# Transposes of the last keys and queries on the way back from DRAM, and first loads behind weight loads

## The chip, the core and the metric

The kernel runs on one core of a Trainium2 chip. The core has five engines with a queue of instructions each: TensorE (PE, with its weight loads PEld), VectorE (DVE), ScalarE (ACT), GpSimd (POOL) and SyncE (SP). Each works through its own queue in order, and they wait for each other by semaphores. The metric is the device time of one execution in microseconds (us).

## The reference, cut to what matters

```
xn = layernorm(x)                                  # x: 1024 x 512
q, k, v = xn @ Wq.T, xn @ Wk.T, xn @ Wv.T          # 32 heads of queries, 8 of keys and values, 128 wide
q, k = rmsnorm(q, q_norm_w), rmsnorm(k, k_norm_w)  # per head
scores = q @ k.T / sqrt(128)                       # 4 heads of queries share one head of keys
attn = softmax(scores + slope[head] * (key - query), causal)
s = (attn @ v) @ Wo.T
gate, up, down = dequantized 4-bit weights         # 512 x 1792, 512 x 1792, 1792 x 512
g = silu((silu(xn @ gate) * (xn @ up)) @ down)
out = x + s * g
```

All of it is computed near float32 accuracy. Where TensorE multiplies in 16 bits, both factors are split into a high and a low part, and three matmuls (high-high, high-low, low-high) are summed (`mm3`, lines 112 to 116). Keys, queries, values and probabilities therefore come as pairs of 16-bit tiles.

## The kernel before, in words

The order of the instructions on every engine is written out by hand: each queue holds what the program issues, in that order. There are four stages: the layer norm and the gated network (to about 207 us), the projections (from 211 us), a stretch in which the last two projections and the first scores of attention take turns (from about 429 us), and attention alone (from about 480 us).

*Projections.* There are twelve, numbered k = 0 to 11: four rounds of one for keys and values of two groups ("kv", lines 695 to 698) and two for queries of one group each ("q"). A group is one head of keys with its four heads of queries. Number 9 is the last for keys and values (groups 6 and 7), number 10 the queries of group 6, number 11 those of group 7. Each goes through 8 tiles of 128 rows: TensorE makes a tile of 128x512, ACT copies it out and sums squares, POOL multiplies by the inverse norm, and DVE splits it into a high and a low half in one 16-bit tile `a16` (`halves`, lines 667 to 682), which has five buffers. A step later SP issues a DMA that transposes this tile from SBUF to SBUF (`transposed`, L686), and two steps after that a plain DMA that stores the transposed tile in DRAM (`store`, L691 for queries into `qd`, L693 for keys into `kd`). Projection 11 differs: its pairs stay in SBUF (`last_pairs`) and are transposed into place when they are needed (`last_queries`, L855).

The weights of projection k + 2 are loaded during projection k, a quarter with each of the tiles 0 to 3 (L509), and ACT takes their squares from tile 5 on (L517). Squares, copies and the weights' own split into high and low (L578 on ACT, L580 on DVE) stand in ACT's one queue in the order of the tiles. Before the first tile of projection 9 the program loads the keys, the values and the first block of queries of group 0 (lines 1140 to 1144).

*Attention.* Per group it goes through blocks of 256 queries, in an order such as 2, 3, 0, 1 (group 0: 3, 2, 1, 0), four heads each, two tiles of 128 queries per head: 256 steps. In a step TensorE makes the scores of one tile (`s<-kT,qT`), and products of probabilities and values (`av<-pT,vT`) and of the output projection (`op`) of earlier steps. DVE adds the bias and finds the minimum (L916), ACT takes exponentials (L922) and the high half (L941), DVE the low half (L950), and SP issues a DMA that transposes the pair from SBUF to SBUF (`split_lo`, L958; L953 for block 0). The values' products come 9 steps after the scores and need the transposed probabilities `pT`. Steps in block 3 transpose 14 and 16 blocks of 128x128, in block 2 10 and 12, in blocks 1 and 0 at most 8.

Keys of the next group are loaded at the fifth step of a group (`load_keys`, L837, 512 KB), values later (`load_values`, L841, 512 KB), and queries block by block ahead of their use (`load_queries`, L845, 512 KB). Weights of the output projection come in quarters (`wor`, L872, 256 KB), are scaled by POOL (L875) and split by ACT (L881) and POOL (L882).

SP issues every DMA of the kernel, loads, stores and transposes. A transpose is issued only when its source is ready, and what stands behind it in SP's queue waits with it. `defer(n, f)` puts an instruction n steps later in this order.

Of the kernel before, what the change touches and what calls it, by code (L numbers as in the profile page):

```python
# [12 lines left out]
F16 = mybir.dt.float16  # L13
# [8 lines left out]
P = 128  # L22
# [3 lines left out]
HKV = 8  # L26
NH = 4
HD = 128
FF = 1792
NI = FF // P  # L30
NT = S // P
# [4 lines left out]
NQT = QB // P  # L36
# [40 lines left out]
def attention_gated_by_ffn_kernel(ctx, tc, x, gu_w, gu_z, gu_s, dn_w, dn_z, dn_s, wq, wkv, wo, qnw, knw, out):  # L77
    nc = tc.nc
    ve, se, ge, te, sp = nc.vector, nc.scalar, nc.gpsimd, nc.tensor, nc.sync

    const = ctx.enter_context(tc.tile_pool(name="const", bufs=1))
    dram = ctx.enter_context(tc.tile_pool(name="scratch", bufs=1, space=DRAM))
# [54 lines left out]
    gsT = const.tile([P, NI, 2, KT], F32, name="gsT")  # L137

    kd = [dram.tile([P, 2, NT, 2 * HD], F16, name=f"kd{i}") for i in range(HKV // 2)]
    vd = [dram.tile([P, NT, 2 * HD], F16, name=f"vd{g}") for g in range(HKV)]  # L140
    qd = [dram.tile([NT, P, 2 * NH * HD], F16, name=f"qd{g}") for g in range(HKV)]
    ald = [dram.tile([1, 2 * HD], F32, name=f"ald{i}") for i in range(HKV // 2)]
# [343 lines left out]
    def finish_step():  # L486

        for f in finishing.pop(clock[0], ()):
            f()
        clock[0] += 1  # L490

    def defer(steps, f):
        finishing.setdefault(clock[0] + steps, []).append(f)
# [4 lines left out]
    class Projection:  # L498
# [168 lines left out]
        def halves(self, t):  # L667
            f = self.f[t // HT][:, t % HT]
            n = self.n
            if self.kind == "q":  # L670
                a16 = fq.tile([P, 2, n, HD], F16, tag="a16", name=f"q16_{self.i}_{t}", bufs=5)
                hi, lo = a16[:, 0], a16[:, 1]
            else:
                a16 = fq.tile([P, 2, 2, HD], F16, tag="a16", name=f"k16_{self.i}_{t}", bufs=5)
                hi, lo = a16[:, :, 0, :], a16[:, :, 1, :]
                ve.tensor_tensor(f, f, wn.unsqueeze(1).to_broadcast([P, 2, HD]), ALU.mult)
            ve.tensor_copy(hi, f)
            ve.tensor_tensor(lo, f, hi, ALU.subtract)
            if self.k == len(projections) - 1:
                last_pairs[t] = a16  # L680
            else:
                defer(1, lambda: self.transposed(t, a16))

# [11 lines left out]
    projections = []  # L695
# [4 lines left out]
    def prepare(k, t):  # L700

        if k < len(projections):
            p = projections[k]
            if t == -1:
                for i in range(p.n + 1):
                    p.squares(i)
            elif t == 1:
                p.norms()
            elif t == 2:
                p.scale()  # L710
            elif t == 6:
                p.factors()
            if 2 <= t < 2 + p.n:
                p.split_head(t - 2)
            elif p.kind == "kv" and 4 <= t < 6:
                p.split_values(t - 4)
# [86 lines left out]
    def queue_half(p, half):  # L803

        last = p is projections[-1]

        def due(steps, i, f):
            if last and i is None:
                c = TILES + LAST_ROOTS[half]
            elif last:  # L810
                c = TILES + LAST_PAIRS[half * HT + i] - 4
            else:
                c = clock[0] + (i or 0)
            finishing.setdefault(c + steps, []).append(f)

        due(0, None, lambda: p.inverse(half))
        if p.by_root:
            due(1, None, lambda: p.root(half))
            due(2, None, lambda: p.newton(half, True))
        else:  # L820
            for i in range(3):
                due((i + 1) // 2, None, lambda i=i: p.newton(half, i == 0))
        later = int(p.by_root)
        for i in range(HT):
            t = half * HT + i
            due(4 + later, i, lambda t=t: p.halves(t))
            due(2 + later, i, lambda t=t: p.normalize(t))

    NB = S // QB
    blocks = [(g, qbs) for g in range(HKV) for qbs in (FIRST_ORDER if g == 0 else ORDER if g < HKV - 1 else LAST_ORDER)]  # L830
    units = [(g, qb, hh) for g, qbs in blocks for hh in range(NH) for qb in qbs]
    kT, vT, qT, woh, wol = {}, {}, {}, {}, {}
    trel, pT, oT, wor = {}, {}, {}, {}

    def load_keys(g):
        kT[g] = ap1.tile([P, NT, 2, P], F16, tag="kT", name=f"kT{g}")
        sp.dma_start(kT[g].rearrange("p t a k -> p t (a k)"), kd[g // 2][:, g % 2])  # L837

    def load_values(g):
        vT[g] = ap1.tile([P, NT, 2, HD], F16, tag="vT", name=f"vT{g}")  # L840
        sp.dma_start(vT[g].rearrange("p t a d -> p t (a d)"), vd[g])  # L841

    def load_queries(g, qb):
        qT[g, qb] = ap1.tile([P, NQT, 2, NH, P], F16, tag="qT", name=f"qT{g}_{qb}", bufs=2)
        sp.dma_start(  # L845
            qT[g, qb].rearrange("p t a g q -> p t (a g q)"), qd[g][qb * NQT : (qb + 1) * NQT].rearrange("t p c -> p t c")
        )
# [11 lines left out]
    def wo_squares_sums():  # L859
        ve.tensor_tensor(rvs, rv, rv, ALU.mult)  # L860
        ve.tensor_tensor(swo16, rvs, swo, ALU.mult)
# [22 lines left out]
    def relative(g):  # L884

        rel = trel[g] = ap1.tile([P, S], F32, tag="trel", name=f"trel{g}")
        if g == 0:
            ge.iota(rel, pattern=[[-1, S]], base=S - P, channel_multiplier=1, allow_small_or_imprecise_dtypes=True)
            ge.affine_select(rel, rel, pattern=[[-1, S]], compare_op=ALU.is_ge, fill=1e20, base=S - P, channel_multiplier=1)
            ge.tensor_scalar(rel, rel, rc, float(SLOPES[NH - 1]), ALU.mult, ALU.mult)  # L890
        else:
            ge.tensor_scalar(rel, trel[g - 1], float(SLOPES[g * NH + NH - 1] / SLOPES[g * NH - 1]), None, ALU.mult)
# [176 lines left out]
    def early_tile(c):  # L1069

        if c % 2 == 0:
            scores(*at(c // 2))
        for stage, lag in ((biased, 1), (exponentials, 2), (split_hi, 5), (split_lo, 6)):
            if (c - lag) >= 0 and (c - lag) % 2 == 0:
                advance(stage, (c - lag) // 2)

    def step(n):
        nonlocal last_ps
        if n < nn:
            u, qt = order[n]  # L1080
            g, qb, hh = units[u]
            for due in q_at.get(n, ()):
                if due[0] < HKV - 1:
                    load_queries(*due)
            for t, due in LAST_QUERIES.items():
                if due == n:
                    last_queries(t)
            if g + 1 < HKV:
                if n % (NB * BS) == KEYS_STEP:
                    relative(g + 1)  # L1090
                    load_keys(g + 1)
                elif n % (NB * BS) == VALUES_STEP:
                    load_values(g + 1)
            scores(u, qt)
# [42 lines left out]
    last_ps = None  # L1137
    relative(0)
    for k, p in enumerate(projections):
        if k == len(projections) - 3:  # L1140
            load_keys(0)
            load_values(0)
            for qb in blocks[0][1]:
                load_queries(0, qb)
        for t in range(NT):
            prepare(k + 1, t)
            if k + 2 < len(projections):
                if t < KT:
                    projections[k + 2].load(t)
                n = projections[k + 2].n  # L1150
                for i in (range(n + 1)[: n // 2], range(n + 1)[n // 2 : n - n // 4], range(n + 1)[n - n // 4 :])[t - 5] if t >= 5 else ():
                    projections[k + 2].squares(i)
            if t == HT:
                p.undo()
            if (k, t) == (len(projections) - 3, HT + 1):
                wo_squares_sums()

            row = t if k < len(projections) - 1 else (t + HT) % NT
            p.tile(row)
            finish_step()  # L1160
            if t % HT == HT - 1:
                queue_half(p, row // HT)
            c = (k - len(projections) + 2) * NT + t
            if c >= 0:
                for due in q_at.get(c // 2, ()) if c % 2 == 0 else ():
                    load_queries(*due)
                if c == 2 * KEYS_STEP:
                    relative(1)
                    load_keys(1)
                early_tile(c)  # L1170
# [46 lines left out]
```

## Time and profile before

| | |
|---|---|
| median of 3 runs | 1058.47 us (1057.25 to 1058.75) |
| the profiled execution | 1057.9 us |
| its span, first to last instruction | 1056.1 us |
| mean granted TensorE clock | 0.989 |
| busy share PE, DVE, ACT, POOL | 95%, 83%, 76%, 40% |
| mean traffic of the DMAs | 195 GB/s, 205.43 MB |
| packets under 512 bytes | 401538 of 456095 |

The profile is of one execution. Times within it count from its first instruction. "Busy" is the time in which an engine works on an instruction, waits not included; for SP the rows are the issues of DMAs ("SPq"), and their duration is the time that the issue took, not the transfer. A line number such as L958 is the line of the kernel; a name such as pT<-p is the tile written and the tile read, and stands for all buffers of that name. The share of the DMAs is the mean busy time of 16 DMA engines; it can be above 1 where packets overlap. The chain of waits follows the work that ended last back from the end, at each step to what released it.

### The profile page before, as it was taken

The numbers are of one execution on the slowest core, as the hardware profiler recorded it, in microseconds if no ns is written. First come the engines' busy times: TensorE is split into PE (matmuls) and PEld (weight loads), VectorE is DVE, ScalarE is ACT, GpSimd is POOL, SyncE is SP. The second block draws the span as 40 slices with busy tenths as digits, with TensorE's granted clock in tenths as the row PEclk, the third lists the DMA queues.
The fourth block names the chain that finished last, engine by engine and source line by source line (L and its number), as shares of the span: only waits on it lengthen the run. The fifth ranks groups of instructions, "written<-read, shape, count | busy, mean of one in ns | idle before, by whom it ended". The sixth has DMA issues, their size and how long they took to land.

```text
span 1056.1 us, 18372 instructions
## 1 busy us (share of the span) xinstructions
PE 1001.2 (95%) x5909; PEld 585.6 (55%) x5909; DVE 878.1 (83%) x1744; ACT 800.9 (76%) x2160; POOL 423.7 (40%) x408
## 2 busy tenths in 40 slices
PE   7899999999999999997899999999999999998996
PEld 4344487744444444444556566567666665665563
DVE  7988997537878886786789898798998989978985
ACT  5777745868887786877779788787987979967772
POOL 2587762125655644461225215113151141340632
PEclk9999999999999999899999999999999999999998
DMA  7123269446999989989999899899999998999995
GB/s 244 60 90 124 75 200 327 148 149 138 243 234 215 258 195 259 225 172 237 200 191 217 187 222 198 165 223 209 187 222 180 227 210 172 232 226 168 236 187 130
DMA packets 456095, 205.43 MB, mean 195 GB/s; under 512 B 401538, under 2 KB 412094, under 8 KB 455998
## 3 DMA queue, kind: packets, MB, share of 16 engines
q1 hardware_dynamic: 455998, 204.26, 87.1%
q8 instruction: 46, 0.75, 0.3%
q14 instruction: 51, 0.42, 0.1%
HBM read 78.37 MB, written 27.27 MB: 100 GB/s over the span
## 4 chain that ended last, share of the span: by engine, by line
PE 63%; DVE 11%; DMA 9%; ACT 9%; issue 6%; POOL 1%; SPq 0%; DVEq 0%; POOLq 0%; ACTq 0%
DMA pT<-p 6%; PE gu_ps L273 5%; PE s L114 4%; PE s L116 4%; PE s L115 4%; PE ps_q L115 4%; PE av L114 4%; PE ps_q L116 4%; PE ps_q L114 4%; PE av L116 4%; PE av L115 4%; PE op L116 4%; PE op L114 4%; PE op L115 4%; PE ps_kv L114 2%
## 5 line engine op out<-in xcount | busy, mean ns | idle before, releaser
L950 DVE SCALAR_TENSOR_TENSOR p<-pf,row,p 128x1024 f16<-128x1024 f32 (+7 forms) x256 | 223.4, 873 | 24.5 <-ACT p L941 21.5
L922 ACT ACTIVATE pf<-pf,row 128x1024 f32<-128x1024 f32 (+7 forms) x256 | 197.4, 771 | 41.1 <-DVE row L916 36.7
L916 DVE CUSTOM_DVE_ANT_0 pf<-s,trel,cs 128x1024 f32<-128x1024 f32 (+7 forms) x256 | 207.0, 809 | 21.3 <-PE s L116 20.7
L941 ACT ACTIVATE p<-pf,row 128x1024 f16<-128x1024 f32 (+7 forms) x256 | 196.6, 768 | 9.5 <-DMA pT<-p 4.6
L114 PE MATMUL av<-pT,vT 128*128 128x256 f16 (+1 forms) x640 | 168.8, 264 | 23.8 <-DMA pT<-p 23.8
L115 PE MATMUL av<-pT,vT 128*128 128x256 f16 (+1 forms) x640 | 168.8, 264 | 0.0
L116 PE MATMUL av<-pT,vT 128*128 128x256 f16 (+1 forms) x640 | 168.6, 264 | 0.0
L114 PE MATMUL s<-kT,qT 128*128 128x512 f16 (+3 forms) x384 | 126.2, 329 | 5.7 <-DVE row L916 5.7
L115 PE MATMUL s<-kT,qT 128*128 128x512 f16 (+3 forms) x384 | 126.0, 328 | 0.0
L116 PE MATMUL s<-kT,qT 128*128 128x512 f16 (+3 forms) x384 | 124.4, 328 | 0.0
L875 POOL TENSOR_SCALAR wor<-wor,rvs 128x512 f32<-128x512 f32 x32 | 51.8, 1618 | 173.2 <-DMA wor<-in_wo 152.6
L115 PE MATMUL ps_q<-wl_q,xth 128*128 128x512 f16 x256 | 98.0, 383 | 3.8 <-DVE wl_q L580 3.8
L114 PEld LDWEIGHTS <-vT 128*128 128x128 f16 x640 | 62.9, 98 | 64.3 <-DMA pT<-p 16.8
L116 PE MATMUL ps_q<-wh_q,xtl 128*128 128x512 f16 x256 | 98.0, 383 | 0.0
L114 PE MATMUL ps_q<-wh_q,xth 128*128 128x512 f16 x256 | 97.8, 382 | 0.0
L114 PE MATMUL op<-woh,oh 128*128 128x512 f16 x248 | 94.8, 382 | 0.0
L116 PE MATMUL op<-woh,ol 128*128 128x512 f16 x248 | 94.7, 382 | 0.0
L115 PE MATMUL op<-wol,oh 128*128 128x512 f16 x248 | 94.6, 382 | 0.0
L984 ACT ACTIVATE oh<-av 128x256 f16<-128x256 f32 x128 | 47.8, 374 | 57.8 <-PE av L116 57.1
L115 PEld LDWEIGHTS <-vT 128*128 128x128 f16 x640 | 63.0, 98 | 42.4 <-issue 4.4
L665 POOL TENSOR_TENSOR f_q<-f_q,inv_q 128x512 f32<-128x512 f32 x64 | 80.1, 1276 | 1.1
L882 POOL TENSOR_TENSOR wol<-wor,woh 128x512 f16<-128x512 f32 x32 | 50.3, 1572 | 62.2 <-ACT woh L881 60.4
(195 smaller groups left out, 2259.6 us busy)
## 6 DMA issues: line engine op xcount, KB each, us to landing
qd<-tr_q SPq DMA_DIRECT2D x56, 256.0 KB, 3.1
qT<-qd SPq DMA_DIRECT2D x28, 512.0 KB, 4.4
wq<-in_wq SPq DMA_DIRECT2D x32, 256.0 KB, 4.1
wo_sq<-in_wo SPq DMA_DIRECT2D x8, 1024.0 KB, 8.4
wor<-in_wo SPq DMA_DIRECT2D x32, 256.0 KB, 3.6
gui<-in_gu_w SPq DMA_DIRECT2D x13, 512.0 KB, 3.5
wkv<-in_wkv SPq DMA_DIRECT2D x16, 256.0 KB, 3.8
vd<-v SPq DMA_DIRECT2D x8, 512.0 KB, 4.7
```

The costliest lines, as they stand in the source:

```text
L114: te.matmul(ps, lhsT=lh, rhs=rh, start=first, stop=False)
L115: te.matmul(ps, lhsT=lh, rhs=rl, start=False, stop=False)
L116: te.matmul(ps, lhsT=ll, rhs=rh, start=False, stop=last)
L273: te.matmul(banks[j][:, k, :], lhsT=w[:, j, ws], rhs=x[:, j, k * 512 : k * 512 + 512], start=x is xth, stop=x is xtl)
L665: ge.tensor_tensor(f, f, ib, ALU.mult)
L875: ge.tensor_scalar(wor[g, i], wor[g, i], rvs[:, g : g + 1], None, ALU.mult)
L882: ge.tensor_tensor(wol[g, i], raw, woh[g, i], ALU.subtract)
L916: ve.tensor_tensor_reduce(p, ps, trel[g][:, S - w :], cs[:, hh : hh + 1], 3e38, ALU.add, ALU.min, least[:, c])
L922: se.activation(p, p, AF.Exp, bias=least[:, c], scale=-1.0, accum_out=total[:, c])
L941: se.activation(p16[u, qt][:, :, 0, :], pf[u, qt], AF.Copy, scale=scale[:, qt : qt + 1])
L950: ve.scalar_tensor_tensor(lo, p, scale, hi, ALU.mult, ALU.subtract)
L984: se.activation(oh, av_ps[u], AF.Copy, scale=1.0 / P_SCALE)
```

## The change

Three places are edited.

1. In `halves`, the pairs of projections 9 and 10 are no longer transposed from SBUF to SBUF. The tile `a16` is stored as it is: that of projection 9 into a new DRAM tensor `kn`, that of projection 10 into `qd[6]`.
2. `load_keys` for groups 6 and 7 issues eight DMAs that transpose out of `kn`, one in each of eight steps, each for 128 keys of one group (2 blocks of 128x128), instead of one plain load. `load_queries` for group 6 issues two transposes of 8 blocks out of `qd[6]` for each block of 256 queries, instead of one plain load.
3. The loads of group 0's keys and of its first queries move from before the first tile of projection 9 to its fifth tile, behind the four weight loads of projection 11. The load of group 0's values moves to the fifth tile of projection 10.

```diff
     kd = [dram.tile([P, 2, NT, 2 * HD], F16, name=f"kd{i}") for i in range(HKV // 2)]
+    kn = dram.tile([NT, P, 2 * 2 * HD], F16, name="kn")
...
             if self.k == len(projections) - 1:
                 last_pairs[t] = a16
+            elif self.k >= len(projections) - 3:
+
+                dst = qd[self.i][t] if self.kind == "q" else kn[t]
+                defer(1, lambda: sp.dma_start(dst, a16.rearrange("p a g d -> p (a g d)")))
             else:
                 defer(1, lambda: self.transposed(t, a16))
...
     def load_keys(g):
         kT[g] = ap1.tile([P, NT, 2, P], F16, tag="kT", name=f"kT{g}")
+        if g // 2 == HKV // 2 - 1:
+            for t in range(NT):
+                defer(t, lambda t=t: sp.dma_start_transpose(kT[g][:, t], kn[t][:, g % 2 * 2 * HD : (g % 2 + 1) * 2 * HD]))
+            return
         sp.dma_start(kT[g].rearrange("p t a k -> p t (a k)"), kd[g // 2][:, g % 2])
...
         qT[g, qb] = ap1.tile([P, NQT, 2, NH, P], F16, tag="qT", name=f"qT{g}_{qb}", bufs=2)
+        if g == HKV - 2:
+            for i in range(NQT):
+                sp.dma_start_transpose(qT[g, qb][:, i].rearrange("p a g q -> p (a g) q"), qd[g][qb * NQT + i])
+            return
...
     for k, p in enumerate(projections):
-        if k == len(projections) - 3:
-            load_keys(0)
-            load_values(0)
-            for qb in blocks[0][1]:
-                load_queries(0, qb)
         for t in range(NT):
...
             if t == HT:
                 p.undo()
+                if k == len(projections) - 3:
+                    load_keys(0)
+                    for qb in blocks[0][1]:
+                        load_queries(0, qb)
+                elif k == len(projections) - 2:
+                    load_values(0)
```

## The prediction

> **What bounds the kernel now.** I read the page's engine line, then the stretches with their granted clock, then TensorE's timeline for its idle times, then the chain of waits around the first of them, and last the timeline of the SP queue, which issues every DMA.
>
> ```profile
> PE 1001.2 (95%) x5909; PEld 585.6 (55%) x5909; DVE 878.1 (83%) x1744; ACT 800.9 (76%) x2160; POOL 423.7 (40%) x408
> ```
>
> TensorE is the bound: 95% busy, so time can come only from its idle times and from stretches at a low clock. The timeline of TensorE has these beside the lines of this change (the bracket is the idle time before the row and what ended it):
>
> ```profile
> 423.94 0.58 PE L115 MATMUL ps_q<-wl_q,xth 128*128 128x512 f16 x1 [3.83 <-DVE wl_q L580]
> 493.33 0.27 PE L114 MATMUL av<-pT,vT 128*128 128x256 f16 x1 [3.25 <-DMA pT<-p]
> 502.17 0.28 PE L114 MATMUL av<-pT,vT 128*128 128x256 f16 x1 [2.75 <-DMA pT<-p]
> 508.74 0.28 PE L114 MATMUL av<-pT,vT 128*128 128x256 f16 x1 [2.80 <-DMA pT<-p]
> 532.35 0.27 PE L114 MATMUL av<-pT,vT 128*128 128x256 f16 x1 [1.22 <-DMA pT<-p]
> 867.01 0.28 PE L114 MATMUL av<-pT,vT 128*128 128x256 f16 x1 [0.81 <-DMA pT<-p]
> 936.41 0.27 PE L114 MATMUL av<-pT,vT 128*128 128x256 f16 x1 [1.47 <-DMA pT<-p]
> ```
>
> The stretches (length, busy time of PE, PEld, DVE, ACT, POOL, then clock, DMA share, GB/s) add a second cost of a stall: the clock after it.
>
> ```profile
> 490.00:500.00 10.00, 6.17 (x37) 3.92 (x35) 5.24 (x12) 5.27 (x10) 2.84 (x3) 0.83 1.06 270
> 500.00:510.00 10.00, 5.03 (x41) 3.82 (x42) 4.45 (x9) 5.29 (x12) 4.95 (x4) 1.00 1.18 173
> ```
>
> The chain of waits (start, duration) shows what is behind the first stall, and the SP queue's timeline why that DMA was late:
>
> ```profile
> 416.15 4.23 DMA wq<-in_wq
> 420.40 0.73 ACT sq_q L517 x2
> 423.19 0.71 DVE wl_q L580
> ```
>
> ```profile
> 402.67 1.08 SPq L837 DMA_DIRECT2D kT<-kd  x1
> 403.80 0.42 SPq L841 DMA_DIRECT2D vT<-vd  x1
> 404.27 0.43 SPq L845 DMA_DIRECT2D qT<-qd  x1
> 404.81 0.40 SPq L509 DMA_DIRECT2D wq<-in_wq  x1
> 405.96 2.96 SPq L686 DMA_TRANSPOSE tr_q<-q  x1
> ...
> 416.15 0.70 SPq L509 DMA_DIRECT2D wq<-in_wq  x1
> ...
> 493.05 2.99 SPq L958 DMA_TRANSPOSE pT<-p  x1
> ...
> 497.19 4.60 SPq L958 DMA_TRANSPOSE pT<-p  x2
> ```
>
> Three loads of 512 KB stand ahead of the four weight loads of the last projection; the transposes behind them take 2.96 us to issue instead of 1.32, the fourth weight load goes out at 416.15, and ScalarE, which reached its squares at 413.95, waits until 420.40. From 450 to 533 the SP queue has hardly a gap, and the transposes of probabilities in it are late: those that DVE finished at 487.6 and 491.8 go out at 497.19 and 502.62, 9.6 and 10.8 us later. TensorE's four stalls from 493 to 513 wait for exactly these.
>
> **What the change does to the queues.** The order on PE, DVE, ACT and POOL is the same in both kernels. On SP, 16 transposes go between 434 and 488 (8 tr_kv, 8 tr_q) while the 16 stores stay, from another tile; three first loads move behind the weight loads (values a projection later); six plain loads (two kT, four qT, 820 to 935) become 16 transposes of 2 blocks (128x128) and 8 of 8 blocks, out of DRAM. They wait for stores that landed over 300 us earlier and for buffers freed as before, so no wait is added but for SP's own time; POOL issues no DMA. The price of an issue is in the rows by line (ns minimum/median/maximum):
>
> ```profile
> L686 SPq DMA_TRANSPOSE tr_q<-q x56: 1246/1324/2962, 259.1 to 486.7; - x56
> L686 SPq DMA_TRANSPOSE tr_kv<-k x32: 1188/1247/2435, 236.7 to 462.6; - x32
> L837 SPq DMA_DIRECT2D kT<-kd x8: 570/574/1079, 402.7 to 890.3; - x8
> ```
>
> **Part 1, weights ahead of first keys: -5.9.** From 402.67, three rounds of weight load, store and transpose (0.57 + 0.52 + 1.37 with gaps) put the fourth weight load at 410.1; landing 4.23 later it is there at 414.3. ScalarE's wait of 6.45 us shrinks to 0.4. TensorE's 3.83 goes, and so does the slow clock behind it: 12 matmuls from 423.94 at 0.43 us apart instead of 0.215, 2.5 us. 6.3 less the 0.4. Keys and queries go out at 412.6 and 413.2, with the 7.5 us that qT took in the old burst they land at 420.7; the first scores are due at 419.74 + 2.6 = 422.3. Cover 1.6 us; if it is gone, the first scores wait by the difference. Values land near 445, wanted at 480: nothing.
>
> **Part 2, 16 transposes out of the SP queue: -10.1.** Behind the SP gap that ends at 450.14 stand 3 tr_kv and 8 tr_q: 3 x 1.30 + 8 x 1.37 = 14.9 us with gaps, more than the 10.8 us of lateness, so the pT transposes go out when DVE is done. Stalls 3.25 + 2.75 + 2.80 + 0.34 (512.84) + 1.22 go, and the clock of 0.83 over 10 us, 1.7: 12.1. ScalarE's three waits of 2.51, 2.51 and 2.64 for POOL's scaled wor in the same place go too, since the wor loads stand in the same queue. Late next is the chain of ACT and DVE: in 480 to 540 they are busy 42.8 and 42.0 us, in 48 us that would be 89% on average, but 510 to 520 has ACT at 9.37 of 10 already, and three small stalls for DVE row L916 stand between 479 and 489 (0.74, 0.68, 0.28). I give back a little more than these 1.7: 2.0.
>
> The Trainium skill's page "TensorE: Matmul & The Clock Gate" (Why this matters for your kernels) allows idle gaps up to about 3 us without a loss of clock. By that rule the stall of 2.56 us at 660.21 would have kept the full clock, and it did not: 660 to 680 was granted 0.91; the gaps of 2.75 and 2.80 kept it. The row decides: a gap near 2.5 us may cost 1.7 us or nothing.
>
> **Part 3, what comes later: +5.0, the unknown.** The SP queue around the loads of keys:
>
> ```profile
> 850.55 8.31 SPq L958 DMA_TRANSPOSE pT<-p  x3
> 858.95 0.54 SPq L845 DMA_DIRECT2D qT<-qd  x1
> 859.58 6.07 SPq L958 DMA_TRANSPOSE pT<-p  x2
> ...
> 926.24 0.80 SPq L845 DMA_DIRECT2D qT<-qd  x1
> 927.15 7.03 SPq L958 DMA_TRANSPOSE pT<-p  x2
> ```
>
> From 841 to 865 and from 912 to 940 SP issues without a break, so lateness carried into these stretches is not worked off, and the stalls at 867.01 and 936.41 wait for their last transposes: their slack is zero. All depends on x, the issue time of a transpose out of DRAM, which no row shows. In group 5 the keys' eight fall between 822.3 and 841.3, 19 us: eight pT at 1.40 are 11.2, two wor and a qT 2.4, free 5.4; needed 8(x + 0.05). In group 6, 891 to 910: 11.2 and 1.5 taken, free 6.3; needed 10(x + 0.05), two of them queries; and right ahead of 927.15 the load of 0.80 becomes two transposes. With x at the plain load's 0.574 the sums are 5.0, 6.2 and +0.4: 0.4 us late. With x at the transposes' 1.25 and 1.32: 5.0 late in group 5, 6.8 + 1.9 = 8.7 in group 6, with clock (1.7 and 2.5, as above) 17.9. The instruction is nearest to the second row, the source and the 2 blocks to the first; 4 and 8 blocks cost nearly alike (1.25, 1.32), so what is paid is the kind of access. I lean to the first and take 0.7: 0.6 + 1.2 + 0.7 = 2.5 us late, plus one clock dip, 1.7. DMA time: the stretch 440 to 450 ran at 0.51 share and 132 GB/s, 2.0 us for 512 KB, six of them 12.1; 96 blocks at 0.15 (14 and 16 blocks go out in 4.5 us back to back) are 14.4. +2.3 over 110 us whose DMA share is already above 1; a third of it, 0.8, on the path. Together 5.0. No gain is likely here; at best the missing 512 KB bursts (pT took 1.96 and 2.58 behind one) make it 0.
>
> The skill's page "DMA: Bandwidth & Descriptors" (Why small descriptors are slow) speaks against this part: SBUF to SBUF escapes, but 256-byte pieces against HBM pay 11 cycles for 8. No row here has a transpose out of DRAM; by it, as an estimate, the 14.4 would be 19.8, and the forecast 1049.3 at the same third.
>
> **Sum.** -5.9 - 10.1 + 5.0 = -11.0 against the profiled execution's 1057.9 (span 1056.1 and 1.8 around it): 1046.9. That execution lies 0.6 under the median of the runs, so 1047.5.
>
> **Rivals.** (1) Slower: a transpose out of DRAM holds SP as long as one in SBUF or longer. For: the kind of instruction, and 32 rows that never fall below 1.19. Against: those 32 have both ends in SBUF. At 1.25 the 17.9 eats the 16.0: 1060.4. It decides from x of about 1.2; at 1.6 it would be 1067. (2) The stalls at 493 to 513 turn into waits for ACT and DVE: the small stalls for DVE row L916 stand just ahead of them. Against: ACT's own waits there come from the SP queue. Then half of part 2: 1052.5. (3) Part 1 does not do what it says: keys or queries of the first block miss 422.3, as SP is 5 to 10 us behind at 402 to 420. Then a wait of some 3 us there: 1050.5.
>
> **How the numbers follow.** Chances: forecast 0.50 (1040 to 1052), rival 1 0.32, rival 2 0.12, rival 3 0.06. Range: low, all of 6.3 and 12.1 with nothing given back, 1040, less 1 for the unknown; high, rival 1's own value, 1061. Left out is mostly x above 1.25 or slow packets, 0.15. Forecast, 2 and 3 are faster by over 0.2% (2.1 us, about what a measurement can tell): 0.68. Rival 1 lies around no change: 0.07 same, 0.25 slower. The likeliest one's own range is 1040 to 1052.
>
> **What would show it.** Right: no idle time of TensorE before the ps_q that stood at 423.94, ScalarE's wait for wq under 1 us; no pT stalls over 1 us between the first av and the second group's; pT issued within 2 us of DVE's end there; rows kT<-kn and qT<-qd as transposes under 0.8 us. Wrong: those rows at 1.2 us or more and stalls of 4 us and more where 867.01 and 936.41 stood, with a clock under 0.95 there; or landings of those transposes far over 4 us.

## The result

The changed kernel takes 1067.05 us (median of 4 runs, 1064.66 to 1070.91), the kernel before beside it 1057.86 us. The ratio is 1.0081 with a 95% interval of 1.0054 to 1.0107: it is 0.8% slower. A second set of runs (run 5 below) gave 1.0071 (1.0043 to 1.0098). The prediction was 1047.5 us with a range of 1039 to 1061: a gain was forecast and a loss came, above the range. The profiled execution took 1064.66 us, the least of the four; its span is 1062.9 us.

The first half of the prediction can be read off the timeline of TensorE after the change. These are its idle times for `pT` (the bracket: us, what ended it), first in the stretch that held the stalls of 2.75 to 3.25 us, then in groups 5 and 6:

```profile
488.03 0.28 PE L114 MATMUL av<-pT,vT 128*128 128x256 f16 x1 [0.36 <-DMA pT<-p]
494.32 0.28 PE L114 MATMUL av<-pT,vT 128*128 128x256 f16 x1 [2.53 <-DMA pT<-p]
517.99 0.27 PE L114 MATMUL av<-pT,vT 128*128 128x256 f16 x1 [1.44 <-DMA pT<-p]
...
838.03 0.28 PE L114 MATMUL av<-pT,vT 128*128 128x256 f16 x1 [1.44 <-DMA pT<-p]
844.35 0.28 PE L114 MATMUL av<-pT,vT 128*128 128x256 f16 x1 [2.54 <-DMA pT<-p]
856.55 0.27 PE L114 MATMUL av<-pT,vT 128*128 128x256 f16 x1 [1.86 <-DMA pT<-p]
862.52 0.27 PE L114 MATMUL av<-pT,vT 128*128 128x256 f16 x1 [1.56 <-DMA pT<-p]
918.44 0.39 PE L114 MATMUL av<-pT,vT 128*128 128x256 f16 x1 [4.34 <-DMA pT<-p]
930.63 0.27 PE L114 MATMUL av<-pT,vT 128*128 128x256 f16 x1 [1.53 <-DMA pT<-p]
936.10 0.27 PE L114 MATMUL av<-pT,vT 128*128 128x256 f16 x1 [1.06 <-DMA pT<-p]
944.50 0.40 PE L114 MATMUL av<-pT,vT 128*128 128x256 f16 x1 [3.99 <-DMA pT<-p]
965.59 0.27 PE L114 MATMUL av<-pT,vT 128*128 128x256 f16 x1 [2.04 <-DMA pT<-p]
```

The stall ahead of `ps_q` at 423.94 is gone altogether, and the early stalls for `pT` shrank from 10.4 to 4.3 us: those of 3.25 and 2.75 us went but for 0.36, those of 2.80 and 1.22 us stayed as 2.53 and 1.44. In the stretch of groups 5 and 6 the kernel before stood idle for `pT` three times, 5.4 us in all: 0.81 and 1.47 us in the prediction's rows, and once more here:

```profile
957.09 0.27 PE L114 MATMUL av<-pT,vT 128*128 128x256 f16 x1 [3.16 <-DMA pT<-p]
```

Now there are nine stalls of 1.06 to 4.34 us, 20.4 us in all. The last of them, at 965.59, is that of 957.09 and no new one. A ruler for all runs below is the start of a group's first scores: group 1's came at 536.7 and now come at 522.4 (-14.3 us); group 5's at 812.9 and now at 799.7 (-13.2 us); the span ends at 1056.1 and now at 1062.9 (+6.8 us). So 13 us were gained by group 5 and 20 us lost behind it.

What holds the transposes of probabilities back is in the rows by line (ns minimum/median/maximum of SP's time for one issue), here for the two new lines and, third, for the queries of group 7, which are transposed out of SBUF:

```profile
L844 SPq DMA_TRANSPOSE kT<-kn x16: 1242/1526/2255, 810.8 to 915.8; - x16
L856 SPq DMA_TRANSPOSE qT<-qd x8: 1254/1300/1338, 867.6 to 935.7; - x8
L868 SPq DMA_TRANSPOSE qT<-q x8: 1231/1282/1808, 949.1 to 1015.9; - x8
```

A transpose out of DRAM holds SP for 1.53 us with 2 blocks and 1.30 us with 8, one of 8 blocks out of SBUF for 1.28; a plain load took 0.57 us (medians). The SP queue ahead of the longest stall:

```profile
903.79 1.65 SPq L971 DMA_TRANSPOSE pT<-p  x1
905.49 1.51 SPq L844 DMA_TRANSPOSE kT<-kn  x1
907.09 2.61 SPq L856 DMA_TRANSPOSE qT<-qd  x2
909.81 2.29 SPq L971 DMA_TRANSPOSE pT<-p  x1
912.14 1.45 SPq L844 DMA_TRANSPOSE kT<-kn  x1
913.64 0.58 SPq L885 DMA_DIRECT2D wor<-in_wo  x1
914.32 1.44 SPq L971 DMA_TRANSPOSE pT<-p  x1
```

and the row of DVE that made the source of the transpose at 914.32 ready:

```profile
901.46 1.00 DVE L963 SCALAR_TENSOR_TENSOR p<-pf,row,p 128x768 f16<-128x768 f32 x1
```

It was ready at 902.5 and is issued 11.9 us later, with no gap in SP's queue in between; TensorE waits for it until 918.44. Over all 56 `pT` transposes of groups 5 and 6 the time from DVE's end to SP's issue was 0.5 us in the median and at most 4.2 us before; now it is 3.8 us and at most 12.0.

Are the DMA engines busier with the new transposes? The stretches of groups 5 and 6 (length; busy time and number of instructions of PE, PEld, DVE, ACT, POOL; clock, share of the DMA engines, GB/s), first before, then after:

```profile
822.00:892.00 70.00, 69.19 (x492) 44.63 (x490) 63.80 (x142) 59.16 (x135) 18.61 (x14) 1.00 1.02 204
892.00:965.00 73.00, 68.37 (x469) 43.48 (x468) 61.37 (x133) 56.96 (x131) 21.28 (x18) 0.98 1.11 217
```

```profile
809.00:887.00 78.00, 70.60 (x484) 44.59 (x483) 62.86 (x140) 58.41 (x135) 16.14 (x14) 0.98 0.93 178
887.00:973.00 86.00, 73.04 (x484) 45.39 (x482) 62.41 (x139) 58.59 (x133) 19.55 (x18) 0.94 0.97 187
```

The same work of DVE (125 us) takes 164 us in place of 143, at a lower DMA share and a lower rate. Nor did the transfers of `pT` take longer: from issue to landing the median in these stretches is 4.2 us before and 4.0 after. That speaks against the transfers and for the queue that issues them, but two traces alone do not settle it. TensorE's own work also took longer, 143.6 us in place of 137.6, at the lower clock.

### The profile page after: what moved, and what is told of

It reads as the page before. It is cut to its first block, busy times and chain, and to the rows that moved or that the text cites. A ratio compares the mean times of both kernels' runs of the same rounds, so it can differ in the third digit from the quotient of the medians.

```text
span 1062.9 us, 18370 instructions
## 1 busy us (share of the span) xinstructions
PE 1002.0 (94%) x5909; PEld 585.4 (55%) x5909; DVE 877.7 (83%) x1744; ACT 800.1 (75%) x2160; POOL 419.6 (39%) x408
## 4 chain that ended last, share of the span: by engine, by line
PE 65%; DMA 10%; DVE 10%; ACT 7%; issue 5%; POOL 2%; SPq 1%; POOLq 0%; DVEq 0%; ACTq 0%
DMA pT<-p 8%; PE gu_ps L274 5%; PE s L115 4%; PE s L114 4%; PE s L116 4%; PE av L114 4%; PE ps_q L114 4%; PE ps_q L115 4%; PE ps_q L116 4%; PE av L116 4%; PE av L115 4%; PE op L115 4%; PE op L114 4%; PE op L116 4%; PE ps_kv L114 3%
## 5 line engine op out<-in xcount | busy, mean ns | idle before, releaser
L963 DVE SCALAR_TENSOR_TENSOR p<-pf,row,p 128x1024 f16<-128x1024 f32 (+7 forms) x256 | 221.1, 864 | 25.5 <-ACT p L954 22.2
L1002 DVE SCALAR_TENSOR_TENSOR ol<-av,oh 128x256 f16<-128x256 f32 x128 | 53.4, 417 | 29.8 <-ACT oh L997 29.8
```

Source lines behind the costliest of these rows:

```text
L963: ve.scalar_tensor_tensor(lo, p, scale, hi, ALU.mult, ALU.subtract)
L1002: ve.scalar_tensor_tensor(ol, av_ps.pop(u), 1.0 / P_SCALE, oh, ALU.mult, ALU.subtract)
```

## The experiments

Theory 1: the late loss is SP's issue time. Twenty-four transposes stand in a queue that also carries the `pT` transposes, and the price goes by the issue. Rival 2: the price goes by bytes or blocks, that is by the DMA engines' time and reads out of DRAM in short pieces. Rival 3: the moved loads and the stores of pairs shift what comes behind them. Rival 4, which came up on the way: an issue costs the same wherever in a group it stands. Runs 1 to 4, 5 to 8 and 9 to 12 each have their own runs of the kernel before beside them (medians 1059.18, 1058.89 and 1059.09 us), and the ratios are to these. A "lead" is by how much earlier than in the profile of the kernel before a point is reached.

**1. First loads moved, nothing else.** Against the kernel before:

```diff
-        if k == len(projections) - 3:
-            load_keys(0)
-            load_values(0)
-            for qb in blocks[0][1]:
-                load_queries(0, qb)
...
+                if k == len(projections) - 3:
+                    load_keys(0)
+                    for qb in blocks[0][1]:
+                        load_queries(0, qb)
+                elif k == len(projections) - 2:
+                    load_values(0)
```

> The kernel before with Part 1 alone: only the first keys, values and queries are loaded later, behind the last weights; no transpose is taken out of the queue. Theory 1 (the late loss is SP's issue time of the 24 transposes out of DRAM, and nothing else): Part 1 pays its early gain and nothing comes later, -4 to -7 us against the kernel before; the stall ahead of ps_q at 423.94 is gone, first av about 6 us earlier, the idle in groups 5 to 7 as before. Rival 2 (DMA time and bytes of these transposes): the same, since there are none here. Rival 3 (the moved loads or the pair stores shift the slots of everything behind them and bring the late loss): the gain is lost by the end, 0 to +5 us.

Measured: 1057.6 us, ratio 0.9974 (0.9944 to 1.0003). The profile agrees with theory 1: first scores 4.9 us earlier, group 5's 4.2 us, end 5.0 us. But the profiled execution (1052.87 us) is one of the fastest of ten; the median gives only 1.6 us, and the interval reaches from a gain of 6 us to nothing, so the size stays open. It contradicts rival 3 as far as it goes: nothing is lost behind group 5.

**2. The queries' half alone.** Against the kernel before:

```diff
+            elif self.k == len(projections) - 2:
+                dst = qd[self.i][t] if self.kind == "q" else kn[t]
+                defer(1, lambda: sp.dma_start(dst, a16.rearrange("p a g d -> p (a g d)")))
...
+        if g == HKV - 2:
+            for i in range(NQT):
+                sp.dma_start_transpose(qT[g, qb][:, i].rearrange("p a g q -> p (a g) q"), qd[g][qb * NQT + i])
+            return
```

> The kernel before with the queries' half alone: 8 early transposes of queries leave the queue, 8 come back in group 6 out of DRAM with 8 blocks of 128 x 128 each (64 blocks in all; the keys of the full change are 16 transposes of 2 blocks, 32 blocks in all). First loads as before, keys as before. Theory 1 (the price goes by the issue, 1.3 us of SP's time each): early gain 5 to 9 us; of the late loss of about 20 us in the full change 8 of 24 issues, so 5 to 8 us; in all -4 to +1 us against before, the lateness of pT<-p in group 5 as before and growing only in group 6. Rival 2 (the price goes by bytes or blocks): 64 of 96 blocks, so 13 us of the 20; in all +4 to +8 us.

Measured: 1051.45 us, ratio 0.9933 (0.9908 to 0.9958), 7.7 us faster in the medians. Group 1's first scores come 8.5 us earlier, group 5's 7.6, the end 7.0 us. The early gain is as expected; the late loss is under 1 us, less than theory 1's 5 to 8 and far from rival 2's 13, although these transposes carry two thirds of the blocks. Why it is so small was not tested apart. They replace four plain loads, and four of the eight are issued in group 5, where SP had 12.6 us without a DMA to issue in the kernel before, against 5.6 us in group 6.

**3. A group's keys in one transpose.** Against the changed kernel (`kn` laid out so that the 16 blocks of a group lie in one row per partition):

```diff
-            for t in range(NT):
-                defer(t, lambda t=t: sp.dma_start_transpose(kT[g][:, t], kn[t][:, g % 2 * 2 * HD : (g % 2 + 1) * 2 * HD]))
+            sp.dma_start_transpose(kT[g].rearrange("p t a k -> p (t a) k"), kn[g % 2].rearrange("p t c -> p (t c)"))
```

> The changed kernel, with the keys of groups 6 and 7 laid in DRAM so that one transpose of 16 blocks brings a group's keys, in place of eight of 2 blocks: the same bytes and blocks, 2 issues in place of 16. Theory 1 (SP's issue time): 14 issues of 1.5 us leave the queue of groups 5 and 6, the late loss falls from 20 us to 5 to 8 us, and the kernel takes 1050 to 1056 us, below the kernel before. Rival 2 (DMA time of the bytes, reads of DRAM): the late loss stays, 1063 to 1069 us, and one long transpose may add a burst. Row to look at: the transpose into kT under 2.5 us of SP's time for 16 blocks under theory 1, about 8 times 1.5 us if the price goes by blocks.

Measured: 1048.72 us, ratio 0.9906 (0.9869 to 0.9942). The same bytes and blocks in 2 issues instead of 16 turn the slower kernel into one 0.9% faster than before, a little better than theory 1's 1050 to 1056 us. The layout of `kn` in DRAM changed with it, but the transfers of `pT` are no faster for it: in the stretch of groups 5 and 6 the median from issue to landing is 4.2 us here and 4.0 in the changed kernel. The row by line and the stretches of groups 5 and 6 of this kernel:

```profile
L845 SPq DMA_TRANSPOSE kT<-kn x2: 3047/3178/3309, 809.3 to 880.9; - x2
```

```profile
813.00:884.00 71.00, 68.94 (x489) 44.26 (x487) 63.62 (x141) 58.44 (x134) 19.23 (x14) 1.00 1.05 196
884.00:958.00 74.00, 66.04 (x466) 42.09 (x464) 59.61 (x133) 56.13 (x129) 22.34 (x18) 1.00 1.09 212
```

Sixteen blocks hold SP for 3.2 us, more than the 2.5 that were expected at most, where eight issues of 2 blocks held it for 12.2. The packets are the same in number and bytes to within 0.2%, as the DMA rows of the changed kernel and of this one show:

```profile
q1 hardware_dynamic: 453854, 201.12, 85.2%
```

```profile
q1 hardware_dynamic: 454430, 201.12, 86.9%
```

Rival 2 falls with this for the keys.

**4. The early half alone.** Against the changed kernel: `kn` (laid out for it) and `qd[6]` come back with plain loads. The transposition of these keys and queries is left out of the computation.

```diff
-            for t in range(NT):
-                defer(t, lambda t=t: sp.dma_start_transpose(kT[g][:, t], kn[t][:, g % 2 * 2 * HD : (g % 2 + 1) * 2 * HD]))
+            sp.dma_start(kT[g].rearrange("p t a k -> p t (a k)"), kn[:, g % 2])
...
-        if g == HKV - 2:
-            for i in range(NQT):
-                sp.dma_start_transpose(qT[g, qb][:, i].rearrange("p a g q -> p (a g) q"), qd[g][qb * NQT + i])
-            return
```

> The changed kernel without its 24 late transposes: the pairs are stored as in it, but the keys of groups 6 and 7 and the queries of group 6 come back with plain loads and stay untransposed (this transposition is left out of the computation). Theory 1 and rival 2 (all of the late loss lies in these 24 transposes): only the early gain stays, 13 to 16 us, so 1041 to 1046 us, and pT<-p is late in groups 5 and 6 no more than in the kernel before. Rival 3 (the late loss comes from shifted loads or stores): most of it stays, 1055 us or more.

Measured: 1043.92 us, ratio 0.986 (0.9815 to 0.9905). The lead at group 5 (13.2 us) is kept to the end (13.8 us). The stores of pairs and the moved loads cost nothing later; all of the loss goes with the 24 late transposes. Rival 3 falls.

**5. The changed kernel again,** beside the runs 6 to 8, without an edit.

> The changed kernel as it is, on the chip of the runs beside it, so that they can be read against it and not only against the kernel before. All theories: 0.5% to 1.1% above the kernel before, 1064 to 1070 us.

Measured: 1065.73 us, ratio 1.0071 (1.0043 to 1.0098), and a profile that follows the first one: -11.9 us at group 5, +7.3 us at the end.

**6. The keys' half alone.** Against the kernel before:

```diff
+            elif self.k == len(projections) - 3:
+                dst = qd[self.i][t] if self.kind == "q" else kn[t]
+                defer(1, lambda: sp.dma_start(dst, a16.rearrange("p a g d -> p (a g d)")))
...
+        if g // 2 == HKV // 2 - 1:
+            for t in range(NT):
+                defer(t, lambda t=t: sp.dma_start_transpose(kT[g][:, t], kn[t][:, g % 2 * 2 * HD : (g % 2 + 1) * 2 * HD]))
+            return
```

> The kernel before with the keys' half alone: the 8 transposes of tr_kv of the last key projection leave the queue, 16 of 2 blocks each out of DRAM come back in groups 5 and 6; first loads and queries as before. Theory 1 (SP's issue time, 16 issues of about 1.5 us in place of two plain loads): little early gain, -2 to 0 us at the first scores of group 5; then 12 to 18 us lost, so +10 to +17 us against before, the dearest of all variants. Rival 2 (price by bytes or blocks: 32 of 96): 7 of the 20 us, so +4 to +7 us.

Measured: 1070.6 us, ratio 1.0114 (1.0059 to 1.0169): 11.7 us slower, the dearest of all, with a third of the blocks and two thirds of the issues. In the profile it leads by 2.6 us at group 5 and trails by 15.0 at the end. Sixteen issues cost 17.6 us, 1.1 us each.

**7. A group's keys in two transposes of 8 blocks.** Against run 3:

```diff
-            sp.dma_start_transpose(kT[g].rearrange("p t a k -> p (t a) k"), kn[g % 2].rearrange("p t c -> p (t c)"))
+            for j in (0, NT // 2):
+                src = kn[g % 2][:, j : j + NT // 2].rearrange("p t c -> p (t c)")
+                defer(j, lambda j=j, src=src: sp.dma_start_transpose(kT[g][:, j : j + NT // 2].rearrange("p t a k -> p (t a) k"), src))
```

> As the run with one transpose of 16 blocks for a group's keys, but two of 8 blocks four steps apart: 4 issues in all. In the trace a pT<-p transpose of 8 blocks takes SP 1.25 us and one of 16 blocks 3.0 us, and the 16-block transposes of keys took 3.05 and 3.31 us. Theory 1 (SP's time is the currency): 4 x 1.3 = 5.2 us in place of 6.4 us, in pieces that stand ahead of less: the same or 1 to 2 us less than with the wide one, 1046 to 1050 us. Rival 2 (bytes): no change against either.

Measured: 1053.57 us, ratio 0.9963 (0.9935 to 0.9992). Faster than before, but some 5 us behind run 3, where the same or less was expected. The issues were nearly as cheap as thought (1.44 us in the median), and at the first scores of group 7 its lead is 5.7 us against 7.2 and 8.4 in the two runs with one transpose. The rest is lost in group 7, where no key is loaded any more. Its cause was not found.

**8. Loads of output weights from POOL's queue.** Against the changed kernel:

```diff
-        sp.dma_start(wor[g, i], wo[(g * NH + i) * HD : (g * NH + i + 1) * HD, :])
+        ge.dma_start(wor[g, i], wo[(g * NH + i) * HD : (g * NH + i + 1) * HD, :])
```

> The changed kernel with all its 24 late transposes, but the 32 loads of output weights (wor<-in_wo, 256 KB each, 0.5 to 1.1 us of SP's time) issued from POOL's queue. Nothing of the transposes or of the bytes changes. Theory 1 (SP's queue has no slack in the steps of groups 5 and 6): 4 to 8 of these loads stand in the queue of each of the groups 5 and 6, 0.7 us each, so 6 to 10 us of SP's time come free there and the late loss shrinks by 5 to 9 us: 1057 to 1062 us. Rival 2 (DMA time of the transposes, reads of DRAM): within 2 us of the changed kernel.

Measured: 1067.12 us, ratio 1.0084 (1.005 to 1.0117), no gain. The edit did two things. From the first `pT` transpose of group 5 to that of group 7 the trace has 159.7 us in place of 164.2, a gain of 4.5; but before group 5 it lost 11.4 us of the lead. The wait for DVE in front of the scores doubled (the groups of instructions, changed kernel first):

```profile
L114 PE MATMUL s<-kT,qT 128*128 128x512 f16 (+3 forms) x384 | 125.4, 327 | 6.0 <-DVE row L929 6.0
```

```profile
L114 PE MATMUL s<-kT,qT 128*128 128x512 f16 (+3 forms) x384 | 125.4, 327 | 12.0 <-DVE row L929 11.7
```

POOL's queue is in order too, and a load there stands behind POOL's own waits; that this is the cause was not tested. The time is 1.4 us from the changed kernel's 1065.73, which is what rival 2 had forecast and theory 1 (1057 to 1062) had not; but two effects of the edit oppose each other. The run speaks for theory 1 only within the stretch, where SP's time and the length both fall (table below).

**9. The keys' part undone.** Against the changed kernel:

```diff
-            elif self.k >= len(projections) - 3:
+            elif self.k == len(projections) - 2:
...
-        if g // 2 == HKV // 2 - 1:
-            for t in range(NT):
-                defer(t, lambda t=t: sp.dma_start_transpose(kT[g][:, t], kn[t][:, g % 2 * 2 * HD : (g % 2 + 1) * 2 * HD]))
-            return
```

> The changed kernel with its keys' part undone: first loads moved, queries out and back as in it, keys transposed early as in the kernel before. Theory 1: the keys' half alone took the queue 16 issues in groups 5 and 6 and gave only 2 to 5 us early, so nearly all of the loss goes with it: the two early gains of the single runs (4 to 5 and 8 us) add up, the 8 query transposes cost 1 to 3 us, and the kernel takes 1045 to 1050 us. Rival 2 (by bytes, the queries being two thirds): 1055 to 1060 us.

Measured: 1046.25 us, ratio 0.9882 (0.9856 to 0.9909), the fastest of those that leave nothing out. The lead is 12.1 us at group 5 and 10.8 at the end. So in this combination the keys' half gave next to nothing early and cost nearly all of the loss; the other two parts are 1.2% faster than the kernel before.

**10. The 16 small transposes of keys 16 steps later.** Against the changed kernel:

```diff
+    QUIET = 20 - KEYS_STEP
...
-                defer(t, lambda t=t: sp.dma_start_transpose(kT[g][:, t], kn[t][:, g % 2 * 2 * HD : (g % 2 + 1) * 2 * HD]))
+                defer(QUIET + t, lambda t=t: sp.dma_start_transpose(kT[g][:, t], kn[t][:, g % 2 * 2 * HD : (g % 2 + 1) * 2 * HD]))
```

> The changed kernel with its 16 small key transposes, none taken away, but issued 16 steps later: at steps 20 to 27 of a group, where the pT<-p of query block 0 come one to every two steps, in place of steps 4 to 11, where the 10- to 16-block ones come one to every step. Theory 1 (it is the place: an issue costs time only where the queue has none to spare): the late loss of 20 us falls to 4 to 9 us, so 1048 to 1055 us. Rival 2 (bytes, reads of DRAM) and rival 4 (the issues cost the same wherever they stand): 1063 to 1069 us.

Measured: 1063.53 us, ratio 1.0042 (1.0029 to 1.0056). It regains 2 to 4 us of the 20 and not 11 to 16: my expectation of theory 1 was wrong here, and rival 4 right (rival 2 had the same number, but run 3 speaks against it). The lead of 8.7 us at group 5 becomes a lag of 7.1 at the end. The place is no quiet one: SP is 2.5 us late when block 3 of group 5 is over (854.4 for a source that was ready at 851.9). In run 9 it works off such a delay in the steps of block 0; here the transposes of keys stand in them, and eight steps later the delay is 8.1 us. Yet in this place one costs less of SP's time:

```profile
L846 SPq DMA_TRANSPOSE kT<-kn x16: 1167/1243/2210, 857.4 to 955.2; - x16
```

**11. The one transpose of 16 blocks, 16 steps later.** Against run 3:

```diff
-            sp.dma_start_transpose(kT[g].rearrange("p t a k -> p (t a) k"), kn[g % 2].rearrange("p t c -> p (t c)"))
+            defer(20 - KEYS_STEP, lambda: sp.dma_start_transpose(kT[g].rearrange("p t a k -> p (t a) k"), kn[g % 2].rearrange("p t c -> p (t c)")))
```

> One transpose of 16 blocks for a group's keys, issued at step 20 of a group in place of step 4. Theory 1: 6 us of SP's time move to steps with room, so the late loss falls below the wide run's 4.7 us: 1 to 3 us faster than that, 1045 to 1049 us. Rival 2: the same as the wide run at step 4.

Measured: 1046.92 us, ratio 0.9885 (0.9858 to 0.9913). Against run 12, the same at step 4, this is within the noise. Its two wide transposes held SP for 1.99 and 4.17 us.

**12. Run 3 again,** beside runs 9 to 11, without a further edit.

> The run with one transpose of 16 blocks at step 4 once more, for an interval beside the other two places and layouts: 1047 to 1051 us, 0.9% below the kernel before.

Measured: 1048.55 us, ratio 0.9902 (0.9878 to 0.9926). The intervals of runs 9, 11 and 12 overlap; which of them is best is not settled.

**The sum over the queue.** Run 10 says that it is not the place but the total. So I added up, from the SP rows of each trace, the issue time of all DMAs from the first `pT` transpose of group 5 to the first of group 7, and set it beside the length of that stretch (us; one profiled execution each):

| kernel | DMA issues | their time on SP | length of the stretch | rest |
|---|---|---|---|---|
| 1, first loads moved | 81 | 124.9 | 142.6 | 17.7 |
| 4, no late transposes | 81 | 125.9 | 142.8 | 16.9 |
| before | 81 | 124.8 | 143.0 | 18.2 |
| 2, queries alone | 85 | 131.9 | 144.9 | 13.0 |
| 12, one transpose per group | 85 | 133.5 | 145.1 | 11.6 |
| 3, the same | 85 | 133.8 | 145.2 | 11.4 |
| 9, keys undone | 85 | 131.0 | 145.6 | 14.7 |
| 11, one per group, later | 86 | 132.5 | 147.3 | 14.8 |
| 7, two per group | 88 | 136.4 | 148.9 | 12.5 |
| 10, small ones later | 100 | 145.6 | 158.7 | 13.1 |
| 8, `wor` on POOL | 92 | 147.8 | 159.7 | 11.8 |
| 6, keys alone | 96 | 144.4 | 160.5 | 16.1 |
| 5, after again | 100 | 149.9 | 163.3 | 13.4 |
| after | 100 | 151.1 | 164.2 | 13.0 |

(In runs 3 and 12 the one transpose of group 6's keys is issued before the stretch begins.) The kernel before already issues for 87% of this stretch. About 6 us of the rest can be filled; what is added beyond that makes the stretch longer nearly one for one: 26.3 us more of SP's time, 21.2 us more length. The 56 `pT` issues in the stretch themselves took 104.8 us before and 100.0 after: the added time is that of the new issues, and not of old ones that became slower. The 4 us that run 10 regains are in the table too: its sixteen issues at 1.24 us in place of 1.53 make SP's time 5.5 us less and the stretch 5.5 us shorter. The table follows theory 1 for issues of 2, 8 and 16 blocks alike.

## Why the prediction was wrong

- *Part 1, -5.9: about right in the profile, its size open in the medians.* The wait ahead of `ps_q` is gone, the first scores come 6.4 us earlier. ScalarE's wait for `wq` did not shrink below 1 us as foretold: the trace has 4.5 us in two pieces between 385 and 425 (6.9 before), without idle time of TensorE behind them. Alone (run 1) the part is worth 5 us in the profile and 1.6 us in the medians.
- *Part 2, -10.1: too large by about 2, and the queries' half gave most of it.* The lead at group 1 is 14.3 us of the 16.0 forecast, 6.4 of which stand at the first scores already, so 7.9 belong here. The stalls did not all go: 2.53, 1.44 and 0.36 us are left, as SP is still 2.5 to 4.7 us late there. I counted 3 `tr_kv` and 8 `tr_q` behind the SP gap that ends at 450.14. But in the kernel before SP had caught up once more at 457.91, where a `pT` transpose went out 0.03 us after DVE's end; only one `tr_kv` stands behind that. The 8 `tr_q` alone (run 2) bring 8.5 us, the `tr_kv` alone (run 6) 5.3 at group 1 and 2.6 by group 5, and without the keys (run 9) the lead is the same 14 us.
- *Part 3, +5.0: the step that failed.* It hangs on x, the issue time of a transpose out of DRAM. I took 0.7, near the plain load, because "the source and the 2 blocks" spoke for that row. Measured: 1.53 us for 2 blocks and 1.30 for 8. In these rows the price goes with the kind of instruction and not with the source: out of SBUF the row of 8 blocks has 1.28 us, out of DRAM 1.30. The row of 32 transposes of keys with 4 blocks at 1.25, which stood in the prediction, was the nearest one, not the plain load. The rest of that sum was sound: with the measured 1.53 and 1.30 it gives about 18 us of lateness and 4.2 of clock, 22 in all, and the traces have 20.0. (One more term was too small: the eight `pT` issues of group 5's window took 12.9 us, where the sum has 11.2.)
- *The prediction's rival 1: this is what happened.* Its value of 1067 for x = 1.6 is met to the microsecond by luck: x was 1.53 and 1.30, for which the same sum gives about 1065. Its chance of 0.32 stood below the forecast's 0.50, and the range ended at its value for 1.25, the lower of the two medians of the transposes' rows, so that any x above that was left out. Of the signs given for "wrong" most came: rows over 1.2 us, a stall of 3.99 us where that of 936.41 stood, and a clock below 0.95 (0.94 in the second stretch above). Where 867.01 stood the stall is 1.56 us, at a clock of 0.98 in the first stretch; the one of 4.34 us came where there was none before. Landings stayed at 2.7 us for keys and 4.4 for queries, which was the part of the sign that pointed to the transfers.
- *DMA time, +0.8: not seen.* The share of the DMA engines fell in groups 5 and 6, as the stretches show. The Trainium skill's page "DMA: Bandwidth & Descriptors" (Why small descriptors are slow) asks 11 cycles in place of 8 for 256-byte pieces against HBM; no run here isolates that. The packets are equal in number and bytes to within 0.2% in the changed kernel and in run 3, with the loss and without it, so it is not what tells these two apart.
- *The prediction's rivals 2 and 3* did not occur: the early idle times that are left end with `pT`, but for the three small ones for DVE ahead of them (0.72, 0.67 and 0.28 us, nearly as before), and the first scores came at 422.2 us, where 422.3 were due.

## What to carry to other kernels

Price a DMA by what it costs the queue that issues it, and not by its bytes: here a transpose of 2 blocks held SP for as long as one of 8, and one of 16 blocks replaced eight of 2 at a quarter of their time. Before a transfer is moved or split, add up the issue time of that queue over the whole stretch: a stall of 1 us can hide a queue that is 87% full. Here some 6 us more could be filled; what came beyond that lengthened the stretch nearly one for one, at both places that were tried. When an edit has several parts, run them apart: here two parts were worth 1.2% and the third took away more than both.

## What the runs showed of the hardware

- SP's time for a transpose hardly depends on its size up to 8 blocks; in the medians it then jumps between 14 and 16. In the changed kernel's trace the `pT` transposes of 6, 8, 10, 12 and 14 blocks have medians of 1.22, 1.25, 1.36, 1.49 and 1.55 us, those of 16 blocks 2.99 us. The least times show no such jump (1.49 us for 14 blocks, 1.79 for 16), and single issues reach 3.7 us with 14 blocks and 4.0 with 16. Six of 16 blocks out of DRAM (runs 3, 11 and 12) took 1.99 to 4.17 us. So the time is not a fixed price; what makes an issue long is open.
- The same small transpose costs SP 1.53 us among the large `pT` transposes and 1.24 us among the small ones (run 10).
- The clock after a gap is not a matter of its length alone. The Trainium skill's page "TensorE: Matmul & The Clock Gate" (Why this matters for your kernels) sets the bound at about 3 us. In the changed kernel a gap of 2.53 us (494.32) kept the full clock (1.00 in the 6 us after it) and one of 2.54 us (844.35) did not, while in run 3 one of 3.17 us (949.9) kept it: the traces show no bound at 3 us. The stretches after the second one of these, and, from run 3, around the third:

```profile
845.00:847.00 2.00, 2.00 (x10) 1.02 (x9) 1.27 (x4) 1.97 (x7) 0.90 (x1) 0.57 1.03 169
847.00:849.00 2.00, 2.00 (x14) 1.55 (x13) 2.00 (x6) 1.07 (x1) 0.72 (x1) 0.58 1.16 302
```

```profile
949.00:951.00 2.00, 1.08 (x7) 0.71 (x8) 1.27 (x3) 1.97 (x6) 0.00 (x0) 1.00 1.20 261
951.00:953.00 2.00, 2.00 (x16) 1.25 (x14) 2.00 (x5) 1.73 (x4) 0.00 (x0) 1.00 0.86 166
```
